# A two-step graph layer on one Trainium2 core: a threshold guess rewritten, one search round fewer, and steps moved between VectorE, ScalarE and GpSimd

## The chip, the cores and the metric

One core of one Trainium2 chip runs the kernel. The metric is device time in microseconds (us). Before the change it is 1347.66 us, the median of 3 runs (1346.17 to 1348.82). Engines are named as the profile names them: PE is TensorE (PEld its weight loads), DVE is VectorE, ACT is ScalarE, POOL is GpSimd, SP is SyncE, which here only issues DMAs.

## The reference, cut to what matters

3327 nodes with 256 features. The layer runs two steps. Each step forms an attention matrix whose rows are cut to the largest probabilities that make up 0.9 of the mass (top-p), and a diffusion along the sparse matrix `adj`:

```python
def _top_p_attention(X, W1, W2, W3):
    q = X @ W1.T @ W2.T
    k = X @ W3.T
    probs = softmax(q @ k.T, axis=-1)
    idx = argsort(-probs)
    sp = take_along_axis(probs, idx)
    keep_sorted = cumsum(sp) - sp < 0.9
    A = probs * mask_from(idx, keep_sorted)
    return A / maximum(A.sum(-1, keepdims=True), 1e-12)

h = maximum(layernorm(x), 0)
R = adj + eye(N);  R = R / R.sum(-1, keepdims=True)
Xf = Xa = h;  Z = 0
for n in range(2):
    A = _top_p_attention(Xa, W1, W2, W3)
    Xf = R @ Xf
    Xa = A @ Xa
    Z = Z + Xf @ U1[n].T + Xa @ U2[n].T
out = x + layernorm(h + Z) * ln_g + ln_b
```

The cut is exact: for each row the kernel must find the value at which the sum of the smaller entries passes 0.1 of the row's total.

## The kernel before, in words

The 3327 rows are 26 tiles of 128. For each tile and step, one row of weights `e` (128 x 3328, the exponentials) is made, cut, and multiplied with the features.

*How the cut is found.* A formula guesses a threshold from the row's moments (`ms`, or `law` in step 1) and its sum `Z`. ACT measures the row against the guess with one or two whole-row passes (`through`, L631 to L633: a Relu or a Sign with a running sum), and the guess is corrected (`measured_once` for step 0, `measured_twice` for step 1). The result, column 16 of the small tile `g`, lies a little above the wanted threshold. DVE then masks the row with it (L729: `w` holds the entries below the guess, `d2` their sum), computes how much must still be dropped (`need`, L730), takes the 8 largest of each of 20 segments (L734), and searches the candidates in rounds of 8 (`ROUNDS`, L739 to L743: a maximum of 8, then those 8 replaced by zero). A running sum (L748), a comparison with `need` (L751) and two small steps give the exact threshold (`at(1)`, L753). A second whole-row pass (L763) sets the entries under it to zero and sums the rest in `ra`, whose reciprocal (L764) scales the product later. Whether the guess was good enough is recorded for every row (`prove`); if any row failed, a second, slower kernel (`search_graph_layer`) runs afterwards.

*The products.* PE transposes `e` in groups of four blocks (L809), ACT copies each group out of PSUM (L811), PE multiplies it with the features (L823). Logits are L600, their exponentials L604 and L608 on ACT. The diffusion uses the sparsity: in step 0 a list of the nonzero blocks of each column is built from `adj` (`listed`, reduced by DVE in L853; `packed` and `gathered` assign the entries beyond four per row to spare places). POOL gathers rows of `adj` (L900) and of the features (L921) by indirect DMAs, five each per tile, and PE multiplies them (L929). `over` is a count that L865 writes and `packed` uses to build a 0/1 matrix `oh` with two DVE steps (L879, L880).

*The order.* Every engine has one queue, worked in order, and the program writes that order out by hand. A tile's turn is cut into seven parts; for each part a string names which pieces of work emit their next instructions. In these strings `m` is the measuring of the next tile (`n` of the one before), `d` the search of the current tile (`c` its end, one turn later), `s` the diffusion product, `w`, `q` and `p` the logits and packing, `g` a gather on POOL, `f` the ending of a finished tile (L953, L458 to L466, L961, L968 to L971), `e` the end of a tile in step 0. Manual dependencies fix this order on PE, ACT, DVE and POOL for the whole kernel, and on SP for step 0.

```python
PLAN = (("gmdsssa", "gmcdsssa", "edawwpg", "gmsdga", "gmspdea", "ohgdawwqg", "gehmgq"),
        ("llcmss", "lnms", "lwwnfd", "lcmdsssgggg", "fdsmwqdf", "llmdf", "lmwdg"))
```

So in step 1 four gathers stand together in the fourth part and one in the last. DMAs that POOL issues (the gathers) are instructions of POOL's queue.

Of the kernel before, what the change touches and what calls it, by code (L numbers as in the profile page):

```python
# [9 lines left out]
F32 = mybir.dt.float32  # L10
# [3 lines left out]
AF = mybir.ActivationFunctionType  # L14
ALU = mybir.AluOpType
# [3 lines left out]
P = 128  # L19
# [4 lines left out]
NP = NT * P  # L24
# [288 lines left out]
BIG = 1.0e30  # L313
# [32 lines left out]
def guess_graph_layer(ctx, tc, x, adj, w1t, w2t, w3t, u1t, u2t, ln_g, ln_b, out, flag):  # L346
# [66 lines left out]
    one = const.tile([P, 8], F32, tag="one", name="one")  # L413
    for k, c in enumerate((1.0, -1.0, 5.0e-4, SQG[1], SQK[1], math.log(10.0), LNY, 1.0e-12)):
        G.memset(one[:, k : k + 1], c)
# [212 lines left out]
    def con(k):  # L628
        return one[:, k : k + 1]
# [5 lines left out]
    def measured_once(r):  # L635
        e, ms = r["e"], r["ms"]


        col = guessed(r, small.tile([P, 17], F32, tag="g", name="g"))
        S.activation(col(4), col(2), AF.Square, bias=con(4))  # L640
        S.activation(col(11), col(4), AF.Identity, scale=ms(5), bias=ms(6))
        S.activation(col(1), col(0), AF.Exp, scale=-1.0, bias=con(5))
        G.tensor_scalar(col(7), col(9), 0.5, None, ALU.mult)
        G.tensor_scalar(col(8), col(9), 0.5 * NP, None, ALU.mult)
        G.tensor_scalar(col(5), col(1), OFFSET[0], None, ALU.mult)
        G.tensor_scalar(col(10), col(9), col(5), 1.0, ALU.mult, ALU.add)
# [7 lines left out]
        S.activation(col(4), oa[:, 1:2], AF.Relu, scale=col(7), bias=col(3))  # L654
# [12 lines left out]

    def measured_twice(r):
# [9 lines left out]
        G.tensor_scalar(col(7), col(3), ms(3), ms(8), ALU.mult, ALU.add)  # L678
        yield
# [11 lines left out]
        G.tensor_scalar(col(8), r["Z"], -0.1, col(4), ALU.mult, ALU.add)  # L691
# [18 lines left out]
        G.tensor_tensor(col(2), col(3), col(2), ALU.subtract)  # L710
        G.tensor_scalar(col(15), d1, col(0), LNBIG, ALU.is_lt, ALU.mult)
        G.tensor_tensor(col(6), col(6), col(15), ALU.add)
        yield
        S.activation(col(16), col(2), AF.Exp, scale=col(11), bias=col(6))  # L714
# [8 lines left out]
    def settle(step, t, r):  # L723
# [40 lines left out]
        V.reciprocal(ra, ra)  # L764
        yield
        V.tensor_tensor(cum[:, :n], dr[:, :n], b, ALU.mult)
# [69 lines left out]
    def listed():  # L836
# [10 lines left out]
        for k, (t, j0, n) in enumerate(pieces):  # L847
            at = ahead
            if k + 1 < len(pieces):
                ahead = asked(*pieces[k + 1])  # L850
            if j0 == 0:
                fm = small.tile([P, NT], F32, tag="fm", name="fm", bufs=2)
            V.tensor_reduce(fm[:, j0 : j0 + n], at[:, :n], AX.X, ALU.max, apply_absolute_value=True)  # L853
            if j0 + n < NT:
                yield
                continue
            V.scalar_tensor_tensor(fm, fm, 0.0, back, ALU.is_gt, ALU.mult)
            V.memset(fm[:, t : t + 1], 0.0)
# [5 lines left out]
            of = small.tile([P, LIST], F32, tag="of", name="of", bufs=2)  # L864
            V.tensor_scalar(of[:, DIRECT:], ls[:, DIRECT:LIST], 0.0, None, ALU.is_gt, ALU.add,  # L865
                            accum_out=over[:, t : t + 1])
            done.append(t)
            yield

    def packed(t):  # L870

        assert t in done
# [3 lines left out]
        S.copy(ls[:, LIST:], pb[:, 0, :1])  # L876
        yield
        ohs[t] = oh = small.tile([P, P], F32, tag="oh", name="oh", bufs=2)
        V.tensor_scalar(oh, place, ov, ls[:, LIST:], ALU.subtract, ALU.is_lt)  # L879
        V.scalar_tensor_tensor(oh, place, ls[:, LIST:], oh, ALU.is_ge, ALU.mult)  # L880

    def gathered(t):
# [10 lines left out]
        V.scalar_tensor_tensor(of[:, :n], place[:, :n], nth, lo, ALU.is_equal, ALU.mult, accum_out=nth)  # L893
        G.tensor_scalar(index[:, t, DIRECT:], nth, -1.0, float(NONE), ALU.mult, ALU.add)
# [88 lines left out]
    live, ohs, acs, xgs, done, early = {}, {}, {}, {}, [], {}  # L983
# [142 lines left out]
    def refetch(t):  # L1126
# [9 lines left out]
    PLAN = (("gmdsssa", "gmcdsssa", "edawwpg", "gmsdga", "gmspdea", "ohgdawwqg", "gehmgq"),  # L1136
            ("llcmss", "lnms", "lwwnfd", "lcmdsssgggg", "fdsmwqdf", "llmdf", "lmwdg"))
# [4 lines left out]
             0: ("mdbb", "mcdbb", "medbwwbp", "mdbb", "gmpdbwwb", "hgdbgbq", "hgq"),  # L1142
             1: ("ggmdsssbb", "gmcdgsssbb", "gedbwwbp", "bmsdg", "gmpdeg", "hgdwwqg", "hgemgqo"),
             2: ("gmdsssa", "gmcdsssga", "gedawwpg", "gmsdga", "gmspdea", "ohgdawwqg", "gehmgq")}
    OPEN = {-1: ("llcmss", "lnms", "lwwnfd", "lcmdsssggggg", "fmgdswqdf", "llmdf", "lmwfdm"),
            0: ("cmssggg", "nms", "wwnfd", "cmdsss", "fdsmgwqdf", "mdf", "mwd"),
            1: ("cmss", "nms", "wwnfd", "cmdsssgggg", "fdsmwqdf", "mgdf", "mwdg")}
# [133 lines left out]
```

## Time and profile before

| | us |
|---|---|
| runs | 1347.66 (1346.17 to 1348.82) |
| the profiled execution | 1349.25 |
| its span | 1347.5 |
| PE waiting, 750 to 800 us (the turn between the steps) | 21.5 of 50 |
| one slot of step 0, L729 to L729, from 402.17 | 24.50 |
| one slot of step 1, from 976.98 | 21.01 |
| L763, L729 (whole-row passes of DVE) | 3.78, 3.72 each on average |
| L633 (whole-row pass of ACT) | 3.07 each |

The share of busy time is an average over stages. The span has a beginning of some 140 us (layer norm, projections, the first lists), step 0 to about 700 us, a turn of some 100 us, step 1 from about 800 us and an end after 1275 us. The granted TensorE clock was 0.98 of full speed over the span and full in both middles. A duration of POOL in the profile is rough; the distance from the start of one instruction to the start of the next is a better measure, and a start and an end tell what it waited through.

### The profile page before, as it was taken

Reading aid. Unit: us, or ns where it says so; the run is one execution under the profiler, and the core shown is the slowest. Engines: PE = TensorE matmul, PEld = TensorE weight load, DVE = VectorE, ACT = ScalarE, POOL = GpSimd, SP = SyncE. Lnnn points to the kernel's source line nnn. Section 1 sums busy time; section 2 is a strip of 40 time slices with the busy share of each in tenths; the row PEclk is TensorE's granted clock in tenths of the full one; section 3 lists DMA queues with packets and bytes.
Section 4 is the critical chain, followed back from the end, with each engine's and each line's share of the span. In section 5 each row is a group of like instructions: output and inputs, shape, how many; then the busy total and the mean of one; then the engine's idle time right before and its main releaser. Section 6 shows DMA issues by size and latency. Waiting matters only on the chain.

```text
span 1347.5 us, 22277 instructions
## 1 busy us (share of the span) xinstructions
PE 1269.8 (94%) x6495; PEld 975.5 (72%) x6495; DVE 1187.0 (88%) x3637; ACT 1080.0 (80%) x2368; POOL 1002.8 (74%) x1399
## 2 busy tenths in 40 slices
PE   5989999999999999999999579999998999999985
PEld 4635777778777787777877457777777777777774
DVE  6867899999999999999991699899998999999993
ACT  5476798888878888888853889899998999999931
POOL 5214888888888888887873588888888888888822
PEclk9999999999999999999999789999999999999988
DMA  8734455454554545545432212121222212122100
GB/s 278 226 124 140 133 146 158 133 159 128 140 158 132 156 135 144 151 135 149 122 105 82 81 48 83 55 90 55 92 77 65 87 56 91 59 86 89 54 20 24
DMA packets 92645, 149.79 MB, mean 111 GB/s; under 512 B 15425, under 2 KB 59072, under 8 KB 92512
## 3 DMA queue, kind: packets, MB, share of 16 engines
q1 hardware_dynamic: 75056, 105.37, 24.7%
q0 software_dynamic: 16640, 42.69, 12.4%
q8 instruction: 54, 0.88, 0.3%
q14 instruction: 79, 0.65, 0.2%
q10 hardware_dynamic: 816, 0.20, 0.1%
HBM read 120.93 MB, written 27.28 MB: 110 GB/s over the span
## 4 chain that ended last, share of the span: by engine, by line
PE 50%; DVE 27%; ACT 14%; POOL 3%; issue 3%; DMA 2%; SPq 0%; POOLq 0%; DVEq 0%; ACTq 0%
PE pa L823 22%; ACT ja L633 7%; PE pl L600 7%; PE pt L809 6%; DVE w L729 5%; PE pr L929 5%; DVE cand L734 4%; DVE e L763 4%; PE pz L942 3%; DVE bb L741 2%; DVE cand L743 2%; DVE x L763 2%; PE pz L1011 2%; ACT eT L811 1%; ACT e L604 1%
## 5 line engine op out<-in xcount | busy, mean ns | idle before, releaser
L823 PE MATMUL pa<-xw,eT 128*128 128x256 f32 x1352 | 323.1, 383 | 3.3 <-DVE s L953 3.3
L633 ACT ACTIVATE ja<-e,g 128x3328 uint8<-128x3328 f32 x106 | 325.8, 3073 | 0.1
L823 PE MATMUL pa<-x,eT 128*128 128x256 f32 x1352 | 322.0, 379 | 0.0
L823 PEld LDWEIGHTS pa<-xw,eT 128*128 128x128 f32 x1352 | 250.5, 190 | 52.0 <-issue 14.4
L823 PEld LDWEIGHTS pa<-x,eT 128*128 128x128 f32 x1352 | 242.8, 190 | 25.5
L734 DVE MAX8 cand<-w 128x8 f32<-128x168 f32 (+1 forms) x1040 | 253.3, 317 | 0.0
L921 POOL DMA_INDIRECT xg<-bx,index x130 | 200.9, 1546 | 52.8 <-issue 24.4
L811 ACT COPY eT<-pt 128x512 f32<-128x512 f32 (+1 forms) x364 | 199.8, 556 | 46.6 <-PE pt L809 45.9
L809 PE MATMUL pt<-ident,e 128*128 128x128 f32 x1144 | 177.0, 277 | 16.8 <-DVE e L760 9.3
L900 POOL DMA_INDIRECT ac<-in_adj,index x130 | 147.8, 1137 | 58.4 <-issue 26.6
L809 PEld LDWEIGHTS pt<-ident,e 128*128 128x128 f32 x1144 | 140.3, 145 | 60.3 <-issue 33.1
L729 DVE SCALAR_TENSOR_TENSOR w<-e,g 128x3328 f32<-128x3328 f32 x44 | 163.4, 3715 | 2.8 <-ACT g L714 2.7
L921 POOL DMA_INDIRECT xg<-vx,index x130 | 133.3, 1025 | 34.1 <-issue 30.0
L763 DVE SCALAR_TENSOR_TENSOR e<-e,rec 128x3328 f32<-128x3328 f32 x40 | 151.3, 3782 | 0.6
L929 PE MATMUL pr<-xg,ac 128*128 128x257 f32 (+1 forms) x520 | 142.4, 398 | 8.2 <-DVE s L1119 6.5
L604 ACT ACTIVATE e<-pl 128x832 f32<-128x832 f32 x132 | 112.9, 859 | 22.4 <-PE pl L600 19.0
L929 PEld LDWEIGHTS pr<-xg,ac 128*128 128x128 f32 x520 | 94.7, 196 | 34.3 <-issue 14.4
L600 PE MATMUL pl<-both,qT 64*128 64x416 f32 x416 | 93.0, 546 | 8.0 <-ACT e L604 4.3
L741 DVE MAX8 bb<-cand 128x8 f32<-128x160 f32 x286 | 92.6, 324 | 6.4
L600 PE MATMUL pl<-after,qT 64*128 64x416 f32 x416 | 95.7, 554 | 0.5 <-ACT e L604 0.5
L853 DVE TENSOR_REDUCE fm<-at 128x4 f32<-128x512 f32 (+1 forms) x133 | 84.3, 634 | 0.3 <-DMA at<-in_adj 0.3
L946 POOL TENSOR_TENSOR sv<-sv,x 128x256 f32<-128x256 f32 x26 | 65.5, 2518 | 13.4 <-ACT sv L945 12.1
(260 smaller groups left out, 2163.4 us busy)
## 6 DMA issues: line engine op xcount, KB each, us to landing
at<-in_adj SPq DMA_DIRECT2D x114, 256.0 KB
cx<-ac SPq DMA_DIRECT2D x26, 384.0 KB
ac<-cx SPq DMA_DIRECT2D x26, 384.0 KB
wide<-in_adj SPq DMA_DIRECT2D x8, 832.0 KB
e<-in_adj SPq DMA_DIRECT2D x6, 832.0 KB
own<-bx SPq DMA_DIRECT2D x26, 128.5 KB
x<-in_x SPq DMA_DIRECT2D x13, 256.0 KB
xr<-in_x SPq DMA_DIRECT2D x26, 128.0 KB
```

What stands on the lines that cost most here:

```text
L600: PE.matmul(pl[:, a, :wd], qT[p, :], keys_of(step, a).rearrange("p a b -> p (a b)")[:, c : c + wd], start=True, stop=True)
L604: S.activation(e.rearrange("p (a n) -> p a n", a=2)[:, :, c : c + wd], pl[:, :, :wd], AF.Exp, accum_out=za[:, n : n + 1])
L633: S.activation(ja, e, f, bias=guess, scale=sign, accum_out=total)
L729: V.scalar_tensor_tensor(w, e, col(16), e, ALU.is_lt, ALU.mult, accum_out=d2)
L734: V.max(cand[:, 8 * s : 8 * s + 8], w[:, s * SEG : min(NP, (s + 1) * SEG)])
L763: V.scalar_tensor_tensor(e, e, at(1), e, ALU.is_ge, ALU.mult, accum_out=ra)
L809: PE.transpose(pt[:, j, :], e[:, (j0 + j) * P : (j0 + j + 1) * P], ident)
L811: S.copy(eT[:, :w, :], pt[:, :w, :])
L823: PE.matmul(self.pa, eT[:, c - 4 * k, :], self.xa[:, j, :], start=c == 0, stop=c == NT - 1)
L900: G.indirect_dma_start(out=ac[:, k, :], out_offset=None, in_=rows, in_offset=bass.IndirectOffsetOnAxis(ap=index[:, t, k : k + 1], axis=0), ...
L921: G.indirect_dma_start(out=xg[:, k, :w], out_offset=None, in_=rows, in_offset=bass.IndirectOffsetOnAxis(ap=index[:, t, k : k + 1], axis=0))
L929: PE.matmul(pr[:, :w], ac[:, k, :], own if k == KT - 1 else xg[:, k, :w], start=k == 0, stop=k == KT - 1)
```

## The change

It replaces the last steps of the guess in both steps of the layer, drops the sixth search round of step 1, and moves small instructions between engines:

- Step 0, `measured_once`: the exponent of the correction is worked out as a logarithm. Two guards and the cap that DVE applied to the finished value (five instructions) become terms ahead of the last Exp (three DVE instructions, then a Relu and an Exp on ACT). Two ACT steps (a Square and a Ln of its result) give way to one Ln. POOL gets four more small instructions. In the order, these guards come one part earlier (`m` from the seventh part to the sixth), ahead of the second whole-row pass of DVE.
- Step 1, `measured_twice`: the exponent is a quadratic of column 11, worked out on POOL beforehand (two instructions); the last steps shrink by two on DVE (L706, L707), two on POOL's final chain, one on POOL before it (L691) and one on ACT. `ROUNDS` is 5 and 5 instead of 5 and 6.
- Step 1, `settle`: `need` (L730) and the reciprocal of `ra` (L764) move from DVE to POOL, the latter as a power of -1.
- Step 0, lists: the count `over` moves from DVE to ACT, as a sum of signs, in a new helper `counted`, with two small POOL instructions per tile. `oh` is made by an ACT Square and one DVE comparison in place of two DVE steps.
- The plan of step 1: the four gathers of the fourth part move to the first three parts, and an ending step `f` from the sixth part to the seventh.

```diff
-ROUNDS = (5, 6)
+ROUNDS = (5, 5)
-OFFSET = (18.0, 14.0)
+OFFSET = (19.0, 24.0)
...
+        G.tensor_scalar(col(11), col(11), -1.0, None, ALU.mult)
         G.tensor_scalar(col(7), col(9), 0.5, None, ALU.mult)
         G.tensor_scalar(col(8), col(9), 0.5 * NP, None, ALU.mult)
         G.tensor_scalar(col(5), col(1), OFFSET[0], None, ALU.mult)
         G.tensor_scalar(col(10), col(9), col(5), 1.0, ALU.mult, ALU.add)
+        G.tensor_scalar(col(12), col(3), ms(3), ms(8), ALU.mult, ALU.add)
+        G.tensor_scalar(col(12), col(12), -1.0, 80.0, ALU.mult, ALU.add)
+        G.tensor_scalar(col(13), r["Z"], 0.035, None, ALU.mult)
...
-        S.activation(col(3), col(4), AF.Square, scale=col(1), bias=con(1))
-        S.activation(col(3), col(3), AF.Ln, scale=0.5, bias=col(10))
-        S.activation(col(3), col(3), AF.Identity, scale=-1.0, bias=col(6))
-        S.activation(col(3), col(3), AF.Exp, scale=col(11))
-        yield
-
-        V.tensor_scalar(col(5), oa[:, 1:2], NP - 31.0, BIG, ALU.is_gt, ALU.mult)
-        V.tensor_scalar(col(6), col(4), col(1), 0.35, ALU.mult, ALU.is_lt)
-        V.scalar_tensor_tensor(col(5), col(6), BIG, col(5), ALU.mult, ALU.add)
-        V.tensor_scalar(col(3), col(3), 1.0e20, col(9), ALU.min, ALU.mult)
-        V.tensor_tensor(col(16), col(3), col(5), ALU.add)
+        S.activation(col(10), col(10), AF.Ln)
+        S.activation(col(10), col(10), AF.Identity, scale=-1.0, bias=col(6))
+        yield
+        V.tensor_scalar(col(5), oa[:, 1:2], NP - 31.0, 60.0, ALU.is_gt, ALU.mult)
+        V.tensor_scalar(col(14), col(4), col(13), 60.0, ALU.is_lt, ALU.mult)
+        V.scalar_tensor_tensor(col(12), col(12), col(5), col(14), ALU.subtract, ALU.subtract)
+        S.activation(col(10), col(10), AF.Relu, scale=col(11), bias=col(12))
+        S.activation(col(16), col(10), AF.Exp, scale=-1.0, bias=con(8))
...
+        G.tensor_scalar(col(12), col(11), -0.4, 0.5, ALU.mult, ALU.add)
+        G.tensor_tensor(col(12), col(12), col(11), ALU.mult)
...
-        G.tensor_scalar(col(8), r["Z"], -0.1, col(4), ALU.mult, ALU.add)
...
-        S.activation(col(2), d1, AF.Abs, scale=col(1), bias=con(1))
-        S.activation(col(2), col(2), AF.Ln, scale=0.2, bias=col(10))
+        S.activation(col(2), col(10), AF.Ln)
         S.activation(col(3), d1, AF.Ln, scale=col(1), bias=con(2))
-
-        V.tensor_scalar(col(12), col(4), d1, 1.0e-30, ALU.subtract, ALU.add)
-        V.reciprocal(col(12), col(12))
-        G.tensor_scalar(col(12), col(12), col(8), 0.7, ALU.mult, ALU.max)
-        G.tensor_scalar(col(11), col(12), 1.5, col(11), ALU.min, ALU.mult)
-        G.tensor_tensor(col(2), col(3), col(2), ALU.subtract)
+        G.tensor_scalar(col(2), col(2), col(12), col(6), ALU.mult, ALU.subtract)
         G.tensor_scalar(col(15), d1, col(0), LNBIG, ALU.is_lt, ALU.mult)
-        G.tensor_tensor(col(6), col(6), col(15), ALU.add)
-        yield
-        S.activation(col(16), col(2), AF.Exp, scale=col(11), bias=col(6))
+        G.tensor_tensor(col(2), col(15), col(2), ALU.subtract)
+        yield
+        S.activation(col(16), col(3), AF.Exp, scale=col(12), bias=col(2))
...
-        V.tensor_scalar(need, Z, -0.1, d2, ALU.mult, ALU.add)
-        yield
+        if not step:
+            V.tensor_scalar(need, Z, -0.1, d2, ALU.mult, ALU.add)
+        yield
+        if step:
+            G.tensor_scalar(need, Z, -0.1, d2, ALU.mult, ALU.add)
...
-        V.reciprocal(ra, ra)
-        yield
+        if not step:
+            V.reciprocal(ra, ra)
+        yield
+        if step:
+            G.tensor_tensor(ra, ra, half[:, 2:3], ALU.pow)
...
-            V.tensor_scalar(of[:, DIRECT:], ls[:, DIRECT:LIST], 0.0, None, ALU.is_gt, ALU.add,
-                            accum_out=over[:, t : t + 1])
...
+    def counted(t):
+
+        if t not in done or t in nhs:
+            return
+        of = small.tile([P, LIST], F32, tag="of", name="of", bufs=2)
+        ov = over[:, t : t + 1]
+        S.activation(of[:, DIRECT:], lists[:, t, DIRECT:LIST], AF.Sign, accum_out=ov)
+        nhs[t] = nh = small.tile([P, 3], F32, tag="nh", name="nh", bufs=4)
+        G.tensor_scalar(nh[:, 0:1], ov, -0.5, 0.5, ALU.mult, ALU.add)
+        G.tensor_scalar(nh[:, 1:2], ov, ov, 0.25, ALU.mult, ALU.mult)
...
+        S.activation(nh[:, 2:3], pb[:, 0, :1], AF.Identity, scale=-1.0, bias=nh[:, 0:1])
         ohs[t] = oh = small.tile([P, P], F32, tag="oh", name="oh", bufs=2)
-        V.tensor_scalar(oh, place, ov, ls[:, LIST:], ALU.subtract, ALU.is_lt)
-        V.scalar_tensor_tensor(oh, place, ls[:, LIST:], oh, ALU.is_ge, ALU.mult)
+        S.activation(oh, place, AF.Square, bias=nh[:, 2:3])
+        yield
+        V.tensor_scalar(oh, oh, nh[:, 1:2], None, ALU.is_lt)
...
-    PLAN = (("gmdsssa", "gmcdsssa", "edawwpg", "gmsdga", "gmspdea", "ohgdawwqg", "gehmgq"),
-            ("llcmss", "lnms", "lwwnfd", "lcmdsssgggg", "fdsmwqdf", "llmdf", "lmwdg"))
+    PLAN = (("gmdsssa", "gmcdsssa", "edawwpg", "gmsdga", "gmspdea", "ohgmdawwqg", "gehmgq"),
+            ("llcmssg", "lnmsg", "lwwnfdgg", "lcmdsss", "fdsmwqdf", "llmd", "lmwfdg"))
```

The strings for the first and last turns (`BEGIN`, `OPEN`) change in the same way.

More of the change, by code (lines that the diff above doesn't have):

```diff
@@ L412, in guess_graph_layer @@
     law = const.tile([P, 7, NT], F32, tag="law", name="law")
-    one = const.tile([P, 8], F32, tag="one", name="one")
-    for k, c in enumerate((1.0, -1.0, 5.0e-4, SQG[1], SQK[1], math.log(10.0), LNY, 1.0e-12)):
+    one = const.tile([P, 9], F32, tag="one", name="one")
+    for k, c in enumerate((1.0, -1.0, 5.0e-4, SQG[1], SQK[1], math.log(10.0), LNY, 1.0e-12, 80.0)):
         G.memset(one[:, k : k + 1], c)
@@ L863, in listed @@
             G.tensor_scalar(index[:, t, :DIRECT], ls[:, :DIRECT], -1.0, float(NONE), ALU.mult, ALU.add)
-            of = small.tile([P, LIST], F32, tag="of", name="of", bufs=2)
-            V.tensor_scalar(of[:, DIRECT:], ls[:, DIRECT:LIST], 0.0, None, ALU.is_gt, ALU.add,
-                            accum_out=over[:, t : t + 1])
             done.append(t)
             yield
+    def counted(t):
[7 more added lines that the diff above has]
+        G.tensor_scalar(nh[:, 1:2], ov, ov, 0.25, ALU.mult, ALU.mult)
     def packed(t):
-        assert t in done
+        counted(t)
+        nh = nhs[t]
         ls, ov = lists[:, t, :], over[:, t : t + 1]
@@ L876, in packed @@
         S.copy(ls[:, LIST:], pb[:, 0, :1])
+        S.activation(nh[:, 2:3], pb[:, 0, :1], AF.Identity, scale=-1.0, bias=nh[:, 0:1])
+        ohs[t] = oh = small.tile([P, P], F32, tag="oh", name="oh", bufs=2)
+        S.activation(oh, place, AF.Square, bias=nh[:, 2:3])
         yield
-        ohs[t] = oh = small.tile([P, P], F32, tag="oh", name="oh", bufs=2)
-        V.tensor_scalar(oh, place, ov, ls[:, LIST:], ALU.subtract, ALU.is_lt)
-        V.scalar_tensor_tensor(oh, place, ls[:, LIST:], oh, ALU.is_ge, ALU.mult)
+        V.tensor_scalar(oh, oh, nh[:, 1:2], None, ALU.is_lt)
     def gathered(t):
@@ L893, in gathered @@
         V.scalar_tensor_tensor(of[:, :n], place[:, :n], nth, lo, ALU.is_equal, ALU.mult, accum_out=nth)
+        if valid(t + 2):
+            counted(t + 2)
         G.tensor_scalar(index[:, t, DIRECT:], nth, -1.0, float(NONE), ALU.mult, ALU.add)
@@ L982, in guess_graph_layer @@
     own_of = {}
-    live, ohs, acs, xgs, done, early = {}, {}, {}, {}, [], {}
+    live, ohs, acs, xgs, done, nhs, early = {}, {}, {}, {}, [], {}, {}
     none = iter(())
@@ L1141, in guess_graph_layer @@
     BEGIN = {-1: ("mba", "mmbba", "mwwbbaa", "bmwwb", "", "", ""),
[L1142 to L1144 removed]
+             0: ("mdbb", "mcdbb", "medbwwbp", "mdbb", "gmpdbwwb", "hgmdbgbq", "hgq"),
+             1: ("ggmdsssbb", "gmcdgsssbb", "gedbwwbp", "bmsdg", "gmpdeg", "hgmdwwqg", "hgemgqo"),
+             2: ("gmdsssa", "gmcdsssga", "gedawwpg", "gmsdga", "gmspdea", "ohgmdawwqg", "gehmgq")}
     OPEN = {-1: ("llcmss", "lnms", "lwwnfd", "lcmdsssggggg", "fmgdswqdf", "llmdf", "lmwfdm"),
             0: ("cmssggg", "nms", "wwnfd", "cmdsss", "fdsmgwqdf", "mdf", "mwd"),
[L1147 removed]
+            1: ("cmss", "nms", "wwnfd", "cmdsssgggg", "fdsmwqdf", "mgd", "mwfdg")}
     OPEN[2] = OPEN[3] = OPEN[1]
```

## The prediction

> **What bounds the kernel now.** I call the stretch from one masking pass (L729, one per row tile) to the next a slot. I read the totals first, then busy time by stage, then who waits for whom, then the timeline of single slots. Totals, share of the span:
>
> ```profile
> PE 1269.8 (94%) x6495; PEld 975.5 (72%) x6495; DVE 1187.0 (88%) x3637; ACT 1080.0 (80%) x2368; POOL 1002.8 (74%) x1399
> ```
>
> The middle of step 0 and of step 1 (stretch, length, then PE, PEld, DVE, ACT, POOL busy, clock, DMA share, GB/s):
>
> ```profile
> 150.00:700.00 550.00, 548.82 (x2921) 433.67 (x2920) 529.03 (x1637) 459.15 (x1136) 463.47 (x527) 1.00 0.50 141
> 850.00:1250.00 400.00, 394.18 (x2024) 306.23 (x2021) 373.27 (x1118) 377.71 (x734) 340.18 (x493) 1.00 0.25 76
> ```
>
> PE is busy for 99.8% and 98.5%, DVE for 96% and 93%. All that PE waited for between 300 and 650 us, and the largest waits of POOL there (total, times, longest):
>
> ```profile
> PE pt L809 <- ACT nth L890: 0.9, 2, 0.6
> ```
> ```profile
> POOL xg L921 <- issue: 14.9, 51, 0.4
> POOL ac L900 <- issue: 14.5, 54, 0.3
> POOL xg L921 <- ACT g L654: 3.0, 1, 3.0
> ```
>
> So PE sets the pace of step 0, and a gain must come from where PE waits. But POOL hardly waits either: its 0.3 us before a gather follows every gather. Why it is only 84% busy and yet never early is seen in the timeline of one slot (start, duration), POOL, then DVE:
>
> ```profile
> 420.39 0.99 POOL L900 DMA_INDIRECT ac<-in_adj,index  x1 [0.27 <-issue]
> 421.39 4.15 POOL L946 TENSOR_TENSOR sv<-sv,x 128x256 f32<-128x256 f32 x1
> 425.70 0.97 POOL L921 DMA_INDIRECT xg<-bx,index  x1 [0.16 <-issue]
> 426.97 4.21 POOL L921 DMA_INDIRECT xg<-bx,index  x1 [0.30 <-ACT za L620]
> ```
> ```profile
> 420.80 4.15 DVE L763 SCALAR_TENSOR_TENSOR e<-e,rec 128x3328 f32<-128x3328 f32 x1
> 426.67 3.68 DVE L729 SCALAR_TENSOR_TENSOR w<-e,g 128x3328 f32<-128x3328 f32 x1
> ```
>
> Whatever POOL starts inside one of DVE's two long passes ends only after the pass: L946 takes 4.15 us (722 ns at its fastest), a gather 4.21 (942 ns). Step 1 is the same, with POOL's last step before the mask, L712, just ahead of the pass:
>
> ```profile
> 993.78 0.19 POOL L712 TENSOR_TENSOR g<-g 128x1 f32<-128x1 f32 x1
> 994.14 1.12 POOL L921 DMA_INDIRECT xg<-vx,index  x1 [0.17 <-issue]
> 994.18 3.69 DVE L763 SCALAR_TENSOR_TENSOR x<-x,rec 128x3328 f32<-128x3328 f32 x1
> 995.68 2.39 POOL L676 TENSOR_SCALAR g<-g,law 128x1 f32<-128x1 f32 x1 [0.43 <-ACT g L675]
> 997.99 3.67 DVE L729 SCALAR_TENSOR_TENSOR w<-x,g 128x3328 f32<-128x3328 f32 x1
> 998.14 3.60 POOL L677 TENSOR_SCALAR g<-g 128x1 f32<-128x1 f32 x1
> ```
>
> L712 ends 0.2 us before L763 starts. One slot in which a fifth gather stood ahead of this chain shows what lateness costs:
>
> ```profile
> 844.49 3.54 POOL L710 TENSOR_TENSOR g<-g 128x1 f32<-128x1 f32 x1
> 848.62 0.39 ACT L714 ACTIVATE g<-g 128x1 f32<-128x1 f32 x1 [2.65 <-POOL g L712]
> 849.04 3.90 DVE L729 SCALAR_TENSOR_TENSOR w<-x,g 128x3328 f32<-128x3328 f32 x1 [0.85 <-ACT g L714]
> ```
>
> The chain is caught by the pass, ACT stands for 2.65 us with the copies that feed PE behind it, and two slots take 21.93 + 22.50 us where 2 x 21.02 is normal: 2.4 us for one gather of 1.26. POOL is a second bound in both steps, and the change loads POOL.
>
> **The change, part by part.** PE's queue is the same, instruction by instruction.
>
> *DVE, relieved.* Step 1, per tile, start to start: a round less (max and replace, 0.78), L706 and L707 (0.33), L730 (0.13), L764 (0.08), scans 8 wide less (0.05): 1.4 us. Step 0: L865 (0.09), one of the two 128x128 passes L879/L880 (0.34), two of L662 to L666 (0.25): 0.7. PE paces these slots, so inside them this is worth only PE's waits. At the end, where the chain runs through DVE for the last two tiles (1274 to 1319 us), it is on the path: -2.4. At the turn between the steps (the chain goes through ACT and DVE with PE idle) I take -1, between 0 and -3.
>
> *ACT.* Step 0 loses L656 to L659 (1.25 us) and gains four small ones (0.29, 0.29, 0.39, 0.39 by L657, L658 and L654), the Sign count (0.4 by L620 with its accumulator), a 128x1 copy with bias (0.27 by L890) and a 128x128 Square (0.27 by L528): +1.05 on some 20.1 busy of 24 (459.15/550), covered; without that cover it would cost its full 1.05. The new Relu waits for DVE's three guards, which now stand ahead of L763 and so end near 420.8 in the slot above, before ACT comes to it near 422.4. Step 1 loses one of L702 to L704 (0.37).
>
> *POOL, step 0.* Six new 128x1 steps per tile: the sign, two for col 12, col 13, two for nh. L643 to L646 take 0.30 from start to start, a dependent pair 0.40: 2.1 us. The slot from 402.17 (24.50 us long) holds 17.8 us of POOL's own pace and 6.7 lost to the two passes (4.15-0.72 and 4.21-0.95). With 2.1 more it needs 26.6 if the loss stays, and 25.1 at best: the least loss shown is 2.6 a pass, where a gather starts just ahead of it and runs on unhindered (994.14, 1.12 of 3.69). POOL's order decides which, and the step that is caught slides with the load, so I take the lower end, 25.1. PE's pace is 23.95 (22 slots from 161.35 to 688.20): +1.15 a slot, +25 in 22 slots. What becomes late is ACT's L653, which needs L644; L646 now ends 2 to 3.5 us before L653 starts, so the first 2.5 us cost nothing: +23. Ends: 0, if POOL has slack that I don't see, and 22 x 2.65 - 2.5 = +56.
>
> *POOL, step 1.* From the end of L677 to the last gather POOL runs 13.41 us without a break (980.73 to 994.14). Out go L691 (0.35) and L708 to L710 (1.04), and 0.14 of gather gaps; in come two for col 12 (0.42, 0.36), the power for ra (0.68 by L466), need (0.35) and the first step of the new chain (0.37): 14.06. The gathers are five as before, moved past L968 to L971 and L676 to L678; the output stores of SP leave some 2.5 us later, which nothing waits for. In the trace L677 ends 7.56 after the start of L763 (973.17 to 980.73), so if the gather again slips in just ahead of L763, the period is 7.5 + 14.06 = 21.56; if it is caught, it restarts 0.83 late (426.97 + 4.21 against the end of L729 at 430.35): 22.4. In the new order L465, L466 and L961 stand between the chain and that gather, so being caught is no rare case; I take the middle, 22.0, +0.96 over 21.02, in 22 slots: +21. Ends: 0 and +31. The two double slots (+2.4, and +3.8 at 997.99) keep only the extra gather itself: -3.
>
> Two sentences from the Trainium skill. "SBUF — State Buffer", Who interferes with whom, says that a DVE pass with two SBUF inputs holds up only GpSimd instructions that read SBUF, so that gathers would pass and step 0 would lose only some 3.4 us a slot and fit; the row of 4.21 us for a gather says otherwise, and I go by it. "Perfetto Trace Analysis", Optimizing Scalar/DVE Operations, warns that moving work between these two engines might not help because they share a port; by it alone the moved steps would be worth nothing either way.
>
> **Sum.** 1347.5 + 23 + 21 - 3 - 2.4 - 1 = 1385 for the span. The profiled execution took 1349.25 (1.75 more than its span) and lay 1.6 above the median, so 1385 stands for the median too.
>
> **Rivals.**
> *POOL keeps up; PE sets the pace and DVE's relief is cashed.* For it: PE is the only engine without gaps, and small steps can hide where POOL is held anyway. Then the double slots go (-6.2), a wait of 0.12 us for L763 in some 20 slots (-2.4), the end (-2.4): 1347.7 - 11 = 1337. It decides if the six steps of step 0 find 2.1 us inside the passes. Against it: POOL's lack of waits.
> *Only one step is bound by POOL.* Only step 0: 1347 + 23 - 9 = 1361; only step 1: 1347 + 21 - 6 = 1362. About 1361.
> *Nothing moves:* PE's pace everywhere, the gains eaten by new waits: 1347.
> *The new guess is off, 40 candidates don't suffice, and the fallback runs,* adding a whole second kernel. The formulas worked through in double precision for all rows leave at most 36 candidates of 40, in both steps; 2%.
>
> **How the numbers follow.** Both steps bound by POOL 0.45 (1385); one 0.22 (1361); PE's pace with gains 0.25 (1337); no change 0.06; fallback 0.02. Slower is 0.45 + 0.22 + 0.02 = 0.69. A measurement of this kernel tells 0.2% (2.7 us) from no change. The likeliest case by itself spans 1361 to 1415 (POOL's upper ends would give 1347.7 + 56 + 31 - 6 = 1428, both seldom at once). The range reaches down to the rival on the other side: 1335 to 1415.
>
> **What would show it.** Right: step 0 slots near 25.1 us and step 1 near 22.0; PE waiting on ACT, and ACT on POOL (L653 for its POOL columns, the last Exp for POOL's chain); DVE idle ahead of L729; still no idle POOL. Wrong: step 0 slots of 24.0 with PE unbroken, or POOL steps that run inside the long passes at full speed. Step 1 slots below 20.9 would refute PE's pace itself.

## The result, and the profile after

The changed kernel takes 1407.2 us (median of 4 runs, 1406.78 to 1412.55), the kernel before 1348.2 in the same comparison: a ratio of 1.0449, 95% interval 1.0422 to 1.0477. The forecast was 1385, slower, with a range of 1335 to 1415. The profiled execution has a span of 1405.3 us against 1347.5 at the same granted clock (0.982), so the 57.8 us are waits and order, not the throttle. Measured from masking pass to masking pass (L729 before, L725 after; slot 4 starts with the fourth), with the prediction's figure beside each part:

| part | before, us | after, us | difference | predicted |
|---|---|---|---|---|
| start, to slot 4 | 161.4 | 165.1 | +3.7 | 0 |
| 22 slots of step 0 | 526.8 (23.95 each) | 559.9 (25.45 each) | +33.0 | +23 |
| turn | 117.9 | 118.7 | +0.8 | -1 |
| 22 slots of step 1 | 468.7 (mostly 21.02) | 496.8 (mostly 22.52) | +28.1 | +18 |
| end | 72.7 | 64.9 | -7.8 | -2.4 |

The last of the 22 slots of step 0 stands apart: it went from 21.9 to 29.4 us, 7.5 of the 33.0, while the other 21 went from 24.05 to 25.26 on average. For the last tile the new count is made only when `packed` needs it (ACT L875 at 706.29, 0.8 us ahead of its use; for the tile before, at 669.58, 12 us ahead), because its list was not ready at the earlier place. Its two POOL steps (`nh`, L877 and L878) so stand behind three gathers and the eight small steps L643 to L650 in POOL's queue. The waits in that slot, 690 to 726 us (total, times, longest):

```profile
ACT nh L888 <- POOL nh L877: 7.0, 1, 7.0
DVE oh L892 <- ACT oh L890: 6.3, 1, 6.3
...
PE pt L811 <- ACT nh L888: 5.3, 1, 5.3
```

The page's totals and its chain of work that ended last:

```profile
PE 1280.2 (91%) x6495; PEld 971.4 (69%) x6495; DVE 1125.2 (80%) x3325; ACT 1086.1 (77%) x2446; POOL 1083.4 (77%) x1582
...
PE 33%; POOL 24%; DVE 19%; ACT 14%; issue 7%; DMA 2%; SPq 0%; POOLq 0%; ACTq 0%; DVEq 0%
```

DVE's busy time fell by 62 us and POOL's rose by 81 (time in which a pass holds POOL counts as busy). POOL, which held 3% of this chain before the change, now holds 24%; PE fell from half of it to a third. Busy time by stage, same stretches and columns as before:

```profile
150.00:700.00 550.00, 532.29 (x2781) 409.55 (x2780) 482.09 (x1444) 455.74 (x1184) 469.30 (x632) 1.00 0.47 136
850.00:1250.00 400.00, 373.19 (x1910) 289.99 (x1908) 327.01 (x923) 348.20 (x677) 345.15 (x475) 1.00 0.23 70
```

PE is down from 99.8% to 96.8% in step 0 and from 98.5% to 93.3% in step 1. Its own waits are 13.9 us in three entries between 300 and 650 us; who is late is seen one engine back. The largest waits of DVE and ACT over the whole span (total, times, longest):

```profile
DVE g L701 <- POOL g L692: 62.0, 22, 5.5
...
ACT g L704 <- POOL g L693: 50.2, 21, 4.9
DVE fm L855 <- DMA at<-in_adj: 47.1, 20, 4.1
...
ACT g L657 <- POOL g L648: 37.9, 19, 2.9
```

Three of the four end with POOL; the third row, a transfer, is followed up in an experiment. (Left out before the last row is ACT's wait for PE at L813, 44.4 us, which was 45.9 before the change.) In step 0 POOL has hardly a gap in which it could catch up. Part of one slot, first POOL and ACT, then DVE:

```profile
508.00 0.41 POOL L648 TENSOR_SCALAR g<-g,ms 128x1 f32<-128x1 f32 x1
508.44 0.29 ACT L657 ACTIVATE g<-oa,g 128x1 f32<-128x1 f32 x1 [2.36 <-POOL g L648]
...
511.82 4.02 POOL L914 DMA_INDIRECT ac<-in_adj,index  x1 [0.30 <-issue]
516.14 4.38 POOL L914 DMA_INDIRECT ac<-in_adj,index  x1 [0.31 <-issue]
```
```profile
511.34 3.68 DVE L762 SCALAR_TENSOR_TENSOR e<-e,rec 128x3328 f32<-128x3328 f32 x1
...
516.02 3.68 DVE L725 SCALAR_TENSOR_TENSOR w<-e,g 128x3328 f32<-128x3328 f32 x1
```

Both passes hold a gather, 4.02 and 4.38 us for work that takes 0.95. In step 1 it is the steps of the row normalisation that are held:

```profile
1134.24 4.03 POOL L466 TENSOR_TENSOR rstd<-rstd,half 128x1 f32<-128x1 f32 x1
1138.37 3.25 POOL L975 TENSOR_SCALAR nm<-mv,rstd 128x1 f32<-128x1 f32 x1
1141.79 1.12 POOL L935 DMA_INDIRECT xg<-vx,index  x1 [0.17 <-issue]
...
1153.78 0.26 POOL L692 TENSOR_SCALAR g<-g 128x1 f32<-128x1 f32 x1
1154.02 0.26 POOL L693 TENSOR_SCALAR g<-g 128x1 f32<-128x1 f32 x1
...
1156.15 0.19 POOL L708 TENSOR_TENSOR g<-g 128x1 f32<-128x1 f32 x1
...
1156.76 4.03 POOL L466 TENSOR_TENSOR rstd<-rstd,half 128x1 f32<-128x1 f32 x1
```
```profile
1137.76 3.68 DVE L725 SCALAR_TENSOR_TENSOR w<-e,g 128x3328 f32<-128x3328 f32 x1
...
1154.08 0.27 DVE L701 TENSOR_SCALAR g<-oa,g 128x1 f32<-128x1 f32 x1 [2.87 <-POOL g L692]
...
1156.67 3.69 DVE L762 SCALAR_TENSOR_TENSOR e<-e,rec 128x3328 f32<-128x3328 f32 x1
```

The loop can be read off: pass L725 ends at 1141.44, POOL works, with no gap above 0.57 us, up to L692, which ends at 1154.04 (12.60 us), DVE goes from L701 to the next pass in 2.59 (1154.08 to 1156.67), and the two passes last 7.29 from 1134.15 to 1141.44. That is 22.52 with the hand-over of 0.04, the slot.

### The profile page after: what moved, and what is told of

Its sections match the earlier page's. It is cut to its first block, busy times and chain, and to the rows that moved or that the text cites. A ratio compares the mean times of both kernels' runs of the same rounds, so it can differ in the third digit from the quotient of the medians.

```text
span 1405.3 us, 22255 instructions
## 1 busy us (share of the span) xinstructions
PE 1280.2 (91%) x6495; PEld 971.4 (69%) x6495; DVE 1125.2 (80%) x3325; ACT 1086.1 (77%) x2446; POOL 1083.4 (77%) x1582
## 3 DMA queue, kind: packets, MB, share of 16 engines
q0 software_dynamic: 16640, 42.69, 11.3%
## 4 chain that ended last, share of the span: by engine, by line
PE 33%; POOL 24%; DVE 19%; ACT 14%; issue 7%; DMA 2%; SPq 0%; POOLq 0%; ACTq 0%; DVEq 0%
PE pa L825 11%; POOL xg L935 9%; PE pl L600 6%; PE pt L811 5%; ACT ja L633 4%; PE pr L943 4%; DVE e L762 4%; DVE cand L733 2%; PE pz L1025 2%; DVE x L762 2%; POOL ac L914 2%; DVE bb L740 2%; DVE w L725 2%; DVE cand L742 1%; PE pz L956 1%
## 5 line engine op out<-in xcount | busy, mean ns | idle before, releaser
L914 POOL DMA_INDIRECT ac<-in_adj,index x130 | 258.7, 1990 | 52.6 <-issue 15.4
L813 ACT COPY eT<-pt 128x512 f32<-128x512 f32 (+1 forms) x364 | 198.2, 552 | 45.0 <-PE pt L811 44.4
L935 POOL DMA_INDIRECT xg<-bx,index x130 | 137.8, 1060 | 45.4 <-issue 21.8
L725 DVE SCALAR_TENSOR_TENSOR w<-e,g 128x3328 f32<-128x3328 f32 x44 | 162.7, 3697 | 3.7 <-ACT g L710 2.5
L762 DVE SCALAR_TENSOR_TENSOR e<-e,rec 128x3328 f32<-128x3328 f32 x40 | 147.3, 3683 | 0.6
L740 DVE MAX8 bb<-cand 128x8 f32<-128x160 f32 x260 | 84.3, 324 | 5.5
L466 POOL TENSOR_TENSOR rstd<-rstd,half 128x1 f32<-128x1 f32 x26 | 84.0, 3232 | 2.2
```

The costliest lines, as they stand in the source:

```text
L725: V.scalar_tensor_tensor(w, e, col(16), e, ALU.is_lt, ALU.mult, accum_out=d2)
L762: V.scalar_tensor_tensor(e, e, at(1), e, ALU.is_ge, ALU.mult, accum_out=ra)
L813: S.copy(eT[:, :w, :], pt[:, :w, :])
L914: G.indirect_dma_start(out=ac[:, k, :], out_offset=None, in_=rows, in_offset=bass.IndirectOffsetOnAxis(ap=index[:, t, k : k + 1], axis=0), ...
L935: G.indirect_dma_start(out=xg[:, k, :w], out_offset=None, in_=rows, in_offset=bass.IndirectOffsetOnAxis(ap=index[:, t, k : k + 1], axis=0))
```

## The experiments

Each kernel ran once, but for the one before, the changed one, and the two with both steps off POOL (5 and 4 runs). Single times carry a few microseconds of doubt (the kernel before lay between 1346.05 and 1352.99 in the runs beside them), and so do sums of slots: four kernels whose step 0 is that of the changed kernel, instruction for instruction (the changed one among them), took 553.1 to 560.4 us for its 22 slots. What is read below is larger than that, or is called open. Step 0 and step 1 stand for the same 22 slots as in the table above.

| kernel | time, us | step 0 | step 1 |
|---|---|---|---|
| before | 1347.7 to 1348.3 | 526.8 | 468.7 |
| changed | 1407.2 | 559.9 | 496.8 |
| step 0 alone changed | 1387.4 | 557.5 | 468.4 |
| step 1 alone changed | 1365.3 | 527.1 | 496.2 |
| before + six idle POOL steps | 1363.4 | 541.8 | 468.7 |
| gathers of step 1 back | 1391.0 | 553.1 | 485.5 |
| column of its own | 1408.8 | 557.5 | 496.0 |
| need and ra back on DVE | 1395.9 | 560.4 | 476.4 |
| step 0's six steps off POOL | 1373.3 | 523.8 | 496.7 |
| both steps off POOL | 1338.0 | 524.0 | 458.5 |
| the same, gathers back | 1340.2 | 526.9 | 459.6 |
| store later in SP's queue | 1402.3 | 551.8 | 496.1 |
| nh's two steps on ACT | 1392.6 | 540.7 | 496.4 |
| four guard steps on DVE | 1388.2 | 539.5 | 496.0 |

### Each step alone

The first kernel keeps `measured_twice`, `settle`, the rounds, the offset and the gather places of step 1 from before; the second keeps `measured_once` and the offset of step 0.

```diff
-ROUNDS = (5, 5)
-OFFSET = (19.0, 24.0)
+ROUNDS = (5, 6)
+OFFSET = (19.0, 14.0)
```

> Only the step 0 part of the change (guess, lists, the earlier guards), step 1 as before with six rounds. In the changed kernel 22 slots of step 0 took 33 us more and the first 161 us 4 more. If each step is slowed by its own POOL load: step 0 slots near 25.4 us, step 1 slots near 21.0, about 1348 + 37 = 1385 us. If the two steps share one cause (a clock, a late start that is carried on), the parts do not add up: well off 1385.

> Only the step 1 part (five rounds, new guess, need and ra on POOL, gathers spread), step 0 as before. In the changed kernel 22 slots of step 1 took 28 us more and the end 8 us less. POOL's load in its own step: step 0 slots near 24.0, step 1 slots near 22.5, about 1348 + 28 - 8 = 1368 us. If the slots of step 1 are long only because step 0 leaves the pipeline late: step 1 slots near 21.0 and under 1348 us.

1387.4 and 1365.3: the two steps lose separately, and each has in it what the whole change has there (557.5 against 559.9, 496.2 against 496.8). The rival in which only one step is bound by POOL falls.

### Six idle POOL steps in the kernel before

```diff
+        ex = small.tile([P, 6], F32, tag="ex", name="ex")
+        for k in range(4):
+            G.tensor_scalar(ex[:, k : k + 1], col(9), 0.5, None, ALU.mult)
...
+        ey = small.tile([P, 2], F32, tag="ey", name="ey")
+        for k in range(2):
+            G.tensor_scalar(ey[:, k : k + 1], half[:, 1:2], 0.5, None, ALU.mult)
```

> The kernel before with six idle 128x1 steps more on POOL per tile of step 0 (four after L646, two ahead of L894), which write to a tile that nobody reads. Nothing else differs: no guard, no ACT step, no DVE step. If POOL is the second bound of step 0, as forecast, 2 us more of it lengthen the slots from 23.95 to some 25 us, about 1348 + 25 = 1373 us (1365 to 1390). If ACT's added steps or its new wait for DVE's guards slow step 0, nothing is to be seen: 1345 to 1352 us.

1363.4, just below the range of 1365 to 1390. Steps whose results nobody reads cost 15 us, all of it in step 0: POOL's time alone slows this kernel, and PE's 99.8% had hidden that POOL was full as well. But it is less than half of what the real six cost, so the size needed an account of POOL, given below.

### Step 1's gathers back in their places

```diff
-            ("llcmssg", "lnmsg", "lwwnfdgg", "lcmdsss", "fdsmwqdf", "llmd", "lmwfdg"))
+            ("llcmss", "lnms", "lwwnfd", "lcmdsssgggg", "fdsmwqdf", "llmdf", "lmwdg"))
```

> The changed kernel with the order of step 1 as before (four gathers in the fourth part, the ending step one part earlier); POOL's steps are the same. If the sum of POOL's steps counts: step 1 slots 22.0 to 22.8 as in the changed kernel (22.52), total 1400 to 1412 us. If the spread of the gathers, which puts four of them ahead of the steps that ACT and DVE wait for, is the cause: step 1 slots back near 21.0 to 21.4, total about 1407 - 28 = 1379 us.

1391.0, between the two theories. With the group of four back, slots are 22.01. What is late there is the step that the prediction named, the end of the chain:

```profile
1141.72 3.74 POOL L707 TENSOR_SCALAR g<-g 128x1 f32<-128x1 f32 x1
...
1145.90 1.10 POOL L935 DMA_INDIRECT xg<-vx,index  x1 [0.17 <-issue]
1147.06 3.29 POOL L677 TENSOR_SCALAR g<-g,law 128x1 f32<-128x1 f32 x1
```

Pass L762 starts at 1141.60 and catches L707; then a gather slips in between the passes and runs through in 1.10 us. The new places bring the chain's end ahead of the pass, but put two gathers (and the two moved steps, L767 and L730) in front of L692, which DVE then waits for, and leave no gather for the passes.

### What in step 0 makes POOL's load cost more

Four kernels each take one suspect away. First the overwrite: L657 writes column 3, which the new L648 reads, so ACT must wait until L648 has read it.

```diff
-        S.activation(col(3), oa[:, 0:1], AF.Identity, scale=-1.0, bias=col(8))
-        S.activation(col(4), oa[:, 1:2], AF.Relu, scale=col(7), bias=col(3))
+        S.activation(col(15), oa[:, 0:1], AF.Identity, scale=-1.0, bias=col(8))
+        S.activation(col(4), oa[:, 1:2], AF.Relu, scale=col(7), bias=col(15))
```

> The changed kernel, but in step 0 the scaled count is written to a column of its own (15) and no longer over column 3, which the new POOL step of column 12 reads. POOL's load is unchanged. In the changed kernel ACT stood 2.1 us a slot for that reader (50.2 us in 21 waits), and the last POOL step that ACT truly needs ends 0.76 us ahead of the reader (507.65 against 508.41 us in one slot). Theory A (the overwrite adds to POOL's lateness): ACT still waits for the two earlier POOL columns, but up to 0.76 us less a slot, step 0 near 24.8 us a slot instead of 25.45: 1407 - 15 = 1392, from 1388 to 1398. Theory B (POOL's load and its gathers alone set the period, the wait is only where the slack shows): the same time within 3 us, 1404 to 1410.

1408.8. The wait that was the largest of ACT's in step 0 is gone by its name, and nothing is gained: theory A falls. (The 50.2 us in 21 waits that the expectation gives for that reader are the row of L704 above, in step 1; its own row is the 37.9 us in 19.) Between 300 and 650 us ACT now waits at two places of this chain for 33.9 us in all, where it was 36.0 in the changed kernel:

```profile
ACT g L666 <- DVE g L665: 18.3, 14, 2.2
ACT g L657 <- POOL g L645: 15.6, 14, 1.5
```

Next, SP's queue. The store L962 waits there for POOL's L960, and 256 KB loads (L845) stand behind it:

```profile
497.01 0.32 SPq L962 DMA_DIRECT2D sx<-sv  x1
497.42 4.68 SPq L845 DMA_DIRECT2D at<-in_adj  x3
```

POOL filled sv from 496.21; three loads went out together behind the store, and DVE stood until 501.06 for the first. The experiment puts the store behind two of the loads.

```diff
+        for args in held:
+            nc.sync.dma_start(*args)
+        held.clear()
...
-        nc.sync.dma_start(sx[t], sv)
+        if t < NT - 1:
+            held.append((sx[t], sv))
+        else:
+            nc.sync.dma_start(sx[t], sv)
```

> The changed kernel, but in step 0 SP issues the store of sv after two of the next 256 KB loads of the adjacency pieces instead of ahead of them; POOL's load is the same. In the changed kernel SP stood 133 us of 350 for the POOL step that fills sv (56 before), the loads behind it went out three at once, and DVE then waited 32 us in 13 waits for a piece. Theory A (POOL's lateness is passed on through SP's queue to these loads and so to DVE, and this adds to what its load costs): DVE's wait for the pieces goes, and step 0's slot falls from 25.45 us toward the 24.63 that six idle POOL steps cost: 1407 - 18 = 1389, from 1382 to 1396. Theory B (POOL's own period is the limit, the wait for the pieces only sits where the slack shows): within 4 us of the changed kernel.

1402.3, far from theory A and just outside the 4 us of theory B; step 0 at 551.8, at the edge of what equal kernels scatter. DVE's wait for the pieces, 31.9 us between 300 and 650, is gone from its list (it waits 24.4 us there for ACT and POOL, at L663 and L664), SP's for sv falls from 133.3 to 32.5, and ACT's for POOL stays:

```profile
SPq L955 <- POOL sv L965: 32.5, 12, 3.1
```
```profile
ACT g L657 <- POOL g L648: 32.1, 14, 2.6
```

So this wait too was mostly a place where lateness showed: 8 us of slots at most, about what equal kernels scatter (7.4). Last, the steps themselves, in two groups and all together:

```diff
-        G.tensor_scalar(nh[:, 0:1], ov, -0.5, 0.5, ALU.mult, ALU.add)
-        G.tensor_scalar(nh[:, 1:2], ov, ov, 0.25, ALU.mult, ALU.mult)
+        S.activation(nh[:, 0:1], ov, AF.Identity, scale=-0.5, bias=half[:, 1:2])
+        S.activation(nh[:, 1:2], ov, AF.Square, scale=0.5)
```

> The changed kernel, but the two POOL steps that prepare nh (0.45 us of POOL a slot) are on ACT. Theory A (past its slack POOL is the limit one for one): 0.45 x 22 = 10 us less, 1397, from 1392 to 1401. Theory B (the loss is shared out evenly, or these two hide where POOL is held by a pass anyway): 1403 to 1410. If they cost more than their length, by waiting for ACT in front of the gathers: below 1390.

```diff
-        G.tensor_scalar(col(11), col(11), -1.0, None, ALU.mult)
-        G.tensor_scalar(col(12), col(3), ms(3), ms(8), ALU.mult, ALU.add)
-        G.tensor_scalar(col(12), col(12), -1.0, 80.0, ALU.mult, ALU.add)
-        G.tensor_scalar(col(13), r["Z"], 0.035, None, ALU.mult)
...
+        V.tensor_scalar(col(11), col(11), -1.0, None, ALU.mult)
+        V.tensor_scalar(col(12), col(3), ms(3), ms(8), ALU.mult, ALU.add)
+        V.tensor_scalar(col(12), col(12), -1.0, 80.0, ALU.mult, ALU.add)
+        V.tensor_scalar(col(13), r["Z"], 0.035, None, ALU.mult)
```

The column of its own goes with it.

> The changed kernel, but the four POOL steps of step 0's guards and sign (1.65 us of POOL a slot) are on DVE, and the scaled count has a column of its own; nh's two steps stay on POOL. Theory A (one for one past the slack): step 0 at 23.95 to 24.1 us a slot, as with all six gone, or at most 0.45 above: 1374 to 1383. Theory B (nh's two, which stand in front of the gathers, carry much of the loss): 1388 or more.

And both groups together:

> The changed kernel, but step 0's six new POOL steps go elsewhere (four small ones to DVE's guards, two to ACT), and the scaled count has a column of its own. Step 1 is as changed. Theory A (POOL bounds step 0, through six steps and the overwrite): slots return to PE's pace, 23.95 us or a little above for DVE's four and ACT's two small steps: 1407 - 33 = 1374, from 1365 to 1380. Theory B (what makes step 0 slow is ACT's added work or the new order of its steps behind DVE's guards): no gain, 1405 or more.

Step 0 took 540.7 without nh's pair, 539.5 without the four, and 523.8 without either: 19.2, 20.4 and 36.1 us less than 559.9. Nearly additive, and all of the loss in the slots, although DVE has four steps more and ACT two. The last slot must be read by itself: it took 21.2, 25.1 and 21.1 us in the three, for 29.4 in the changed kernel. So 8.3 of the pair's 19.2 us are the one stall shown above. In the other 21 slots the pair gave back 10.9 us (0.52 a slot), the four 16.0 (0.76), all six 27.7 (1.32). Measured from start to start, with the gaps between them, the pair adds 0.47 us a slot to POOL's work and the four 0.99, not the 1.65 of the expectation. Both groups so pay about their length; equal kernels scatter by 6.3 us over these 21 slots, so no more can be told. By its time the kernel without the pair (1392.6) lies in theory A's range and the one without the four (1388.2) in theory B's, but these runs reached slot 4 5.5 and 4.6 us later than the changed kernel, and the pair's large share is the stall. Without the six, PE is whole again in step 0, and step 1 as slow as changed:

```profile
150.00:700.00 550.00, 547.71 (x2921) 434.13 (x2920) 521.30 (x1618) 483.65 (x1270) 459.42 (x530) 1.00 0.48 141
850.00:1250.00 400.00, 373.55 (x1908) 289.18 (x1907) 328.10 (x915) 347.94 (x671) 346.37 (x474) 1.00 0.23 70
```

### Step 1's added steps off POOL

```diff
-        if step:
-            G.tensor_scalar(need, Z, -0.1, d2, ALU.mult, ALU.add)
...
-        if step:
-            G.tensor_tensor(ra, ra, half[:, 2:3], ALU.pow)
```

Both are on DVE for both steps, as before the change.

> The changed kernel, but in step 1 the candidates' need and the reciprocal of ra are on DVE again as before. POOL's run of work loses 0.35 + 0.68 us a slot, and nothing of it stands between the two long passes any more except the step that normalises; DVE gains about 0.21 us a slot. Theory A (POOL's order against the passes sets the 22.52 us slot; the late steps are the two in the middle of the new guess): the power and its step, which the long pass held for 4.03 us, go, and slots fall to 21.0 to 21.6: 1407 - 20 to 33, 1374 to 1387. Theory B (the place of the gathers alone sets it): within 5 us of the changed kernel, 1402 to 1410.

Slots of 21.60, 20.4 us less in step 1, as theory A has it; the time, 1395.9, lies between the two theories and shows 11.3 of it, mostly because this run reached slot 4 7.9 us later than the changed kernel. No run adds idle steps to step 1, so the length of the moved steps and their place ahead of L692 are not told apart there. The next kernel does this, takes the six of step 0 off POOL, and moves column 12's two steps of step 1 to DVE:

```diff
+        V.tensor_scalar(col(12), col(11), -0.4, 0.5, ALU.mult, ALU.add)
+        V.tensor_tensor(col(12), col(12), col(11), ALU.mult)
```

> The kernel of step 0 off POOL, and in step 1 the need, the reciprocal of ra and the two steps of column 12 on DVE too, so that POOL has less to do than in the kernel before. The places of the gathers stay as changed. Theory A (POOL is the whole cause of the loss): both steps at PE's pace, with the double slots and the end gained: 1337 to 1348, at or below the kernel before. Theory B (the gathers' new places cost by themselves about half of step 1's loss): 1352 to 1362.

1338.0 us, ratio to the kernel before 0.9931, interval 0.9908 to 0.9953: theory A, and a version that beats both kernels.

```profile
150.00:700.00 550.00, 547.68 (x2913) 433.78 (x2913) 520.63 (x1613) 483.00 (x1268) 459.89 (x531) 1.00 0.49 141
850.00:1250.00 400.00, 399.78 (x2069) 315.24 (x2068) 364.62 (x1068) 378.49 (x735) 357.43 (x443) 1.00 0.25 76
```

PE is busy for 99.9% of step 1 with slots of 20.87, below the 21.02 of before, and just under the 20.9 that the prediction held for PE's limit. The passes still hold POOL, now a small step and a gather, and nobody is late for it:

```profile
1122.33 3.69 POOL L969 TENSOR_SCALAR nm<-mv,rstd 128x1 f32<-128x1 f32 x1
1126.19 4.46 POOL L929 DMA_INDIRECT xg<-vx,index  x1 [0.16 <-issue]
```

> The kernel with POOL relieved in both steps (1337.96 us), but with step 1's gathers in one group of four again, as before the change. Theory A (the gathers' places matter only where POOL is late): within 4 us, 1334 to 1342, a little more if the two double slots come back (some 6 us, 1344). Theory B (spreading the gathers helps by itself, since a group of four holds up what stands behind it): 1348 or more. With POOL's full load the group of four was better by 16 us.

1340.2, ratio 0.9937, interval 0.9914 to 0.9960: with POOL relieved, the gathers' places make no difference that these runs can tell (the intervals overlap). With POOL's full load the group of four was better by 11 us in step 1's slots.

## Why the prediction was right, and where it was short

**POOL as the second bound: right, and shown.** Loading POOL with idle steps slows the kernel (in step 0, where it was tried), unloading it brings the time below that of before, and no wait that was removed by itself (the overwrite, the store) gave back more than 5 us of the time.

**Step 0, +33 for +23: the slot came out near the forecast by luck, and two terms beside it were put at nothing.** In 21 of the 22 slots the mean was 25.26 us, for 25.1. The missing 10 us are the 2.5 of "the first 2.5 us cost nothing" and the 7.5 of the last slot, whose late pair of steps I did not foresee. The way to 25.1, "the least loss shown is 2.6 a pass ... so I take the lower end", does not hold, as an account of POOL's time per slot shows. I take each line's 25th percentile duration as its own pace, what an instruction lasts beyond that as held by a pass, and what lies between instructions as gap (usual for that pair) or idle (beyond the usual); these are means over the 22 slots, the last one included, worked out from the traces:

| kernel | slot | own pace | gaps | held | idle |
|---|---|---|---|---|---|
| before | 23.95 | 13.77 | 3.43 | 6.48 | 0.27 |
| idle steps added | 24.63 | 14.92 | 3.05 | 6.52 | 0.15 |
| without the four | 24.52 | 14.24 | 3.43 | 6.64 | 0.22 |
| without nh's pair | 24.58 | 14.57 | 3.31 | 6.53 | 0.17 |
| without the six | 23.81 | 13.68 | 3.37 | 6.30 | 0.45 |
| changed | 25.45 | 15.35 | 3.40 | 6.39 | 0.31 |

The four columns add up to the slot by construction; what they show is which of them moves. What the passes take from POOL stays at 6.3 to 6.6 us a slot whatever its load is, and the idle time of before was 0.27. So POOL was already full, and its added 1.58 us became 1.50 us of slot. The last slot left out, the six steps add 1.46 us from start to start and the slot grew by 1.21; the six idle ones add 0.94 and the slot grew by 0.74: in both cases the length, less about the idle time of before. I had seen both ends, 26.6 and 25.1. The high one was built on a slot that was 24.50 us long rather than the mean of 23.95, and on 2.1 us for the six steps where some 1.5 was seen; the low one supposed a loss that fell to 5.2, where it stayed at 6.4. Too much load and too little loss cancelled. "The first 2.5 us cost nothing" was wrong because a lead of one step over its reader is no slack where the whole queue is full.

**What becomes late.** The prediction named L653 of the kernel before, for its POOL columns. ACT did wait at that instruction (L657 now), though most often for the reader of the overwritten column, a dependence that I did not see in the diff; removed, the wait moved on and the time stayed. DVE's wait for the 256 KB pieces, through SP's queue, was not foreseen either, and taking it away gave no more than the scatter. The wait that did cost by itself is the one for `nh` in the last slot.

**Step 1, +28 for +18: the term "whether the gather slips in, 21.56, or is caught, 22.4; I take the middle".** Neither happened, and the size was that of being caught: 22.52. The two passes hold L466 and L975 (4.03 and 3.25 us for 0.58 and 0.26), and no gather lies inside them. Before, the held stretch of 7.61 us (1124.04 to 1131.65) had a gather, L676 and L677 in it; now 7.38 us (1134.24 to 1141.62) have only two small steps, and the rest of the slot, 15.14, is POOL's unbroken run, where it was 13.41. Of these 1.73, the prediction's change of load gives 0.65; the rest is mostly work that used to pass under cover. The last step of the chain, named as the late one, was in time (L708 ends at 1156.34, the pass starts at 1156.67); L692 and L693 in its middle were late, behind two gathers and the two moved steps. The double slots did keep an extra, 25.09 + 22.52 where two are 45.04: 2.57, not the 1.26 of the gather alone.

**The end, -7.8 for -2.4.** The last slot took 19.14 us instead of 22.13, and from the last masking pass to the last accumulating pass it was 17.34 instead of 20.42 (1359.56 to 1376.90, 1296.97 to 1317.39): DVE no longer stood 2.00 us for PE there, and had a round less (0.78). I had counted DVE's own relief only; why PE is no longer late at this place was not tried. The last 1.7 us lie after it and are not explained.

**The start, +3.7 for 0.** All kernels with the new step 0 reach slot 4 at 165.0 to 173.0 us, those with the old one at 160.6 to 163.0. Taking the six steps off POOL does not change that (167.8 and 170.9), so it is not POOL's load. Which part of the new order does it was not tried.

**The rivals.** "PE sets the pace and DVE's relief is cashed", 1337, is what the kernel with POOL relieved gives, 1338.0: the relief was there, and POOL's load hid it. The sum fits better than its parts: that kernel's start is 9.6 us later than before the change, and its end 6.7 us shorter, where the rival had 0 and 2.4. The fallback did not run.

**Gathers under the passes, and steps moved between the two engines.** The gathers above took 4.02 and 4.38 us under the passes and 0.95 to 1.12 outside. The Trainium skill, "SBUF — State Buffer", Who interferes with whom, names only GpSimd instructions that read SBUF as held by a DVE pass with two SBUF inputs. The use of it that I weighed, that gathers would pass, is contradicted by these rows; the gathers here take their row numbers from the tile `index` in SBUF, so the sentence itself may cover them.
Moving four steps from POOL to DVE took 20.4 us off step 0's slots (4.3 of them in the last one), and moving two took 20.4 off step 1's. "Perfetto Trace Analysis", Optimizing Scalar/DVE Operations, says that moving work between GpSimd and DVE might not help, since they share a read port; here it did.

## What to carry to other kernels

An engine that shows 74% busy and no idle time is full: add up its own pace, what other engines hold of it, and its gaps, over many slots and not in one, and if nothing is left, price each added instruction at its full length. When waits appear at several places after a change, remove the load and not the waits; of the two waits taken away alone, each came back at the next place. Read the first and last rounds of a loop by themselves: here one late pair of steps in the last slot cost a quarter of step 0's loss. A relief on one engine is only worth having if the work does not land on one that is full: the same five rounds and logarithms took 10 us less than the kernel before with POOL's steps put on DVE and ACT, and 59 us more with them on POOL.

## What the runs showed of the hardware

What the two long passes take from POOL in step 0 hardly depends on its load (6.3 to 6.6 us a slot in six kernels). Gathers (4.02, 4.38 and 4.46 us for 0.95) and steps of 128x1 (3.25 and 4.03 for 0.26 and 0.58) are held alike until the pass has ended: of 102 POOL instructions in the changed kernel that started inside such a pass, 99 ended after it, and the other three had started within 0.08 us of the pass. A gather that starts just ahead of a pass or between two runs through (1.10 to 1.12). The caught gathers ended 0.82 us after the pass in step 0 (511.82 + 4.02 against 511.34 + 3.68; 516.14 + 4.38 against 516.02 + 3.68). Steps of 128x1 with no reader still cost: six of them, 15 us in 22 slots.
